# A row scale spread by two DMAs instead of transposes, plain stores in an unused path, and an earlier last block

## The chip, the cores and the metric

The kernel runs on one core of one Trainium2 chip, in float32. The metric is the device time of one execution in microseconds (us). Engines are named as in the profile: PE is TensorE, with PEld its weight loads, DVE is VectorE, ACT is ScalarE, POOL is GpSimd and SP is SyncE, which here only issues DMAs.

## The reference

Four sequences of 1024 tokens, D = 256, go through two residual blocks.

```python
x = x + _layernorm(attn_block(_layernorm(x)))
x = x + _layernorm(ffn_block(_layernorm(x)))

# attn_block
h = layer_norm(x, ln1)
q = softmax(h @ wq * scale, axis=-1)      # 4 heads of 64
k = softmax(h @ wk * scale, axis=-2)      # over the 1024 tokens
x = x + (q @ (k.T @ (h @ wv))) @ wo + bo
h = layer_norm(x, ln2)
x = x + gelu(h @ w_ff1 + b_ff1) @ w_ff2 + b_ff2
return x @ w_d + b_d

# ffn_block: nx = RMS norm of x, 8 experts, rank 16, the best 2 per token
weights = top-2 of softmax(nx @ gate.T), made to sum to 1
h1, h3 = nx @ w1.T + 2 * lora1_e(nx), nx @ w3.T + 2 * lora3_e(nx)
out = sum over experts of weight_e * ((silu(h1) * h3) @ w2.T + 2 * lora2_e(...))
```

## The kernel before

**Tiling.** The 4096 tokens are 8 blocks of 512 (BLK). A block is 4 tiles (TB) of 128 tokens, so that a tile `[128, 4, D]` holds token p, t. Two blocks make one sequence. The attention half runs per block; then tokens are scattered into DRAM rows sorted by the pair of experts that each chose, and the expert half runs over 8 groups of 512 such rows: one of kind H, six of kind F, one of kind G (n = 0 to 7). In the profiled run the attention half takes about the first 440 us, H ends near 500, the F groups near 900 and G near 972.

**Who sets the order.** The order of PE, DVE, ACT and POOL is written by the kernel itself, at build time (`manual_schedule`). The work is cut into streams, Python generators: `prelude(i)` loads a block and takes its norms, `front(i)` makes q, k and v, `middle(i)` (L846) does the residual, the second norm and the feed-forward layer, `tail(i)` (L1063 is in it) routes the tokens and scatters the rows, `prepare(n)` and `experts(n)` do an expert group. A small clock model stands beside them: `mm` and `flip` add the PE time of a matmul or transpose, `V`, `A` and `G` add a planned duration to DVE, ACT and POOL and return the planned end, and `psum` hands out the PSUM tile that is free first. A stream yields either the time at which it can go on or a condition; `side()` then picks among those that can. So a changed due time can reorder instructions far away. SP isn't part of this: its DMAs stand on one queue in an order that the framework sets, and a DMA that waits holds those behind it.

**The second norm in `middle(i)`.** After attention, `pa` is added to x1 on DVE and its mean and variance are taken; `rsqrt` (L344 on) adds eps on DVE (L348) and takes the power on POOL (L351), which gives r, one scale for each token, as a `[128, 4]` tile: tokens on partitions. The feed-forward matmuls `pf` need the norm's output with tokens along the free axis. So x1 is transposed on PE, eight flips `pt_h` (L326), which ACT copies to `x1T` in SBUF (L901). The scale of a token must then stand along the free axis on all 128 partitions: four more flips, of r broadcast along its free axis, give the PSUM tile `prb` of 128x512 (L907 to L909), and DVE multiplies (L911), twice 128x512 with one input in PSUM:

```python
prb = psum(f"prb_{i}")
for j in range(TB):
    flip(prb[:, j * P : (j + 1) * P], r[:, j : j + 1].to_broadcast([P, P]))
for c in range(DC):
    nc.vector.tensor_tensor(h2T[:, c, :], x1T[:, c, :], prb, ALU.mult)
```

A gate at L886 lets block i start its flips when block i - 2 has finished its feed-forward matmuls (`fed`), for block 7 when block 6 has, since `x1T_7` lies in the buffer "copy" of a pool with one buffer. After `pf` and gelu (L936) come the output matmuls `py`, whose result is evicted on DVE (L961).

**Other DMAs of that part.** SP loads the blocks (x at L851, z at L176), fills the DRAM rows with a default in four DMAs (`rows<-none`, L838, during block 0), and stores the routed tokens a second time into `kept` (L1127). POOL issues the indirect scatters of rows (`scatter`, L1158). In `prepare(n)` there is a pair of DMAs close to the one that the change adds: 12 rows of 128 routing values are stored to a DRAM scratch `lines` (L1206), and one of its lines is spread over 128 partitions (L1210).

**The end.** The last expert group's four output tiles go through `last` (L1448 on): for each tile j, `measured(j)` takes the norm's statistics on DVE, the power on POOL (L1463) and subtracts the mean on DVE; `stored_(j)` scales and adds the residual on DVE (L1470) and scatters the tile to the output from POOL. It is called for tiles 0 and 1 together, then for 2, then for 3 (L1652 to L1661), so that POOL's order is power 0, power 1, store 0, store 1, power 2, store 2, power 3, store 3.

**The general path.** The groups have fixed sizes. If the counts of expert pairs don't fit them, a flag is set (`have`, `both` at L978 to L980, `lack` and `short` at L1138, L1139, `flag` at L1878), and a loop under `tc.If(lacking > 0)` (L1881 on) does the expert half again on `kept`, block by block, with all experts. With these inputs it isn't taken. It is built all the same, with its own instructions for every engine, and uses `store` (L1544) and its POOL scatters.

Of the kernel before, what the change touches and what calls it, by code (L numbers as in the profile page):

```python
# [15 lines left out]
P = 128  # L16
# [10 lines left out]
TB = 4  # L27
# [39 lines left out]
def sandwich_kernel(  # L67
# [40 lines left out]
    rows = dr.tile([ROWS, RW], F32, tag="rows", name="rows")  # L108
    kept = dr.tile([NBLK * BLK, RW], F32, tag="kept", name="kept")

    lines = dr.tile([NBLK + 1, 3, BLK], F32, tag="lines", name="lines")


# [729 lines left out]

    SPARE = (2, 3, 6)
    AFTER = {4: 0, 5: 1, 6: 2, 7: 4}
    fed, turned, flipped, tails = set(), set(), set(), []  # L846

    def middle(i):
        pool, tag = (sp, "row") if i in SPARE else (xp, "x")
        xt = xts[i] = pool.tile([P, TB, RW], F32, tag=tag, name=f"x_{i}")  # L850
        nc.sync.dma_start(out=xt[:, :, 0:D], in_=tokens(x, i))  # L851
        yield now() + 2.5 if i > 1 else ARRIVE["x"]
        yield lambda: i in norms and (i - 1 in flipped if i > 1 else i == 0 or folded)
        _, r, e = rsqrt(norms[i], 1e-5, f"x{i}")
        pool, tag = (mp1, "actB") if i == 1 else (x1p, "x1")
        x1 = pool.tile([P, TB, D], F32, tag=tag, name=f"x1_{i}", bufs=1)
        yield e
        lm, e = less_mean(norms[i], r, f"x{i}")
        for j in range(TB):
            nc.scalar.activation(  # L860
                x1[:, j, :], xt[:, j, 0:D], AF.Identity, bias=lm[:, j : j + 1], scale=r[:, j : j + 1]
            )
            xe = A(0.45, e)
        nc.gpsimd.iota(xt[:, :, R_ID], pattern=[[1, TB]], base=i * BLK, channel_multiplier=TB,
                       allow_small_or_imprecise_dtypes=True)
        G(0.6)
        yield lambda: i // BPB in mixes and i in qTs
        qT, mix = qTs[i], mixes[i // BPB]
        st, mv = tiles(f"x1_{i}")
        for jj in range(0, TB, 2):  # L870
            pa = psum(f"pa_{i}_{jj}")
            for j in (jj, jj + 1):
                for c in range(DC):
                    mm(pa[:, (j - jj) * D : (j - jj + 1) * D], qT[:, c, j * P : (j + 1) * P],
                       mix[:, c, :], c == 0, c == DC - 1)
            x2 = x1[:, jj : jj + 2, :]
            nc.vector.tensor_tensor(x2, x2, pa.rearrange("p (t d) -> p t d", d=D), ALU.add)
            e = read_out(V(0.69, max(xe, now() + 0.2)))
            e = stats(x1, st, mv, (jj, jj + 1), e)
            yield 0.0  # L880
        attended.add(i)
        _, r, re = rsqrt(mv, 1e-5, f"x1_{i}", e)


        aside = {1: "u0", 3: "act", 5: "act"}.get(i)
        yield lambda: aside != "u0" or 2 in keyed and 3 in summed  # L886
        yield lambda: i < 2 or (i - 2 if i < 7 else i - 1) in fed
        yield lambda: aside != "act" or ranked.done

        if aside == "act":  # L890
            both = mp1.tile([P, 2 * DC, BLK], F32, tag="actA", name=f"x1T_{i}")
            x1T, h2T = both[:, 0:DC, :], both[:, DC : 2 * DC, :]
        else:
            (pool, tag), (pool2, tag2) = (
                ((mp2, "u0"), (mp2, "tT")) if i == 1 else ((mp1, "copy"), (bp, "h2T"))
            )
            x1T = pool.tile([P, DC, BLK], F32, tag=tag, name=f"x1T_{i}")
            h2T = pool2.tile([P, DC, BLK], F32, tag=tag2, name=f"h2T_{i}")

        def to_x1(c, pt):  # L900
            nc.scalar.copy(x1T[:, c, :], pt)  # L901

        for te in transposed(x1, f"h2_{i}", to_x1):
            yield 0.0
        flipped.add(i)
        yield re
        prb = psum(f"prb_{i}")  # L907
        for j in range(TB):
            flip(prb[:, j * P : (j + 1) * P], r[:, j : j + 1].to_broadcast([P, P]))  # L909
        for c in range(DC):  # L910
            nc.vector.tensor_tensor(h2T[:, c, :], x1T[:, c, :], prb, ALU.mult)  # L911
            e = V(0.69, max(te, now() + 0.2))
        yield read_out(e)
        yield lambda: i > 0 or once.done
        W = BLK // 2
        for hf in range(2):
            ts = slice(hf * W, (hf + 1) * W)
            gs = []
            if aside == "act":
                four = mp1.tile([P, FC // 2, BLK], F32, tag="actB", name=f"g_{i}_{hf}")  # L920
            for fp in range(FC // 2):
                pf = psum(f"pf_{i}_{hf}_{fp}")
                if aside == "act":
                    g = four[:, fp, :]
                else:
                    pool, tag = (mp2, ("yacc", "wt")[fp % 2]) if i == 1 else (gp, "g")
                    g = pool.tile([P, BLK], F32, tag=tag, name=f"g_{i}_{hf}_{fp}")
                gs.append(g)
                for k in range(2):
                    f = 2 * fp + k  # L930
                    for c in range(DC):
                        mm(pf[:, k * W : (k + 1) * W], wff1_s[:, c, f * P : (f + 1) * P],
                           h2T[:, c, ts], c == 0, c == DC - 1)
                for k in range(2):
                    f = 2 * fp + k
                    nc.scalar.activation(  # L936
                        g[:, k * W : (k + 1) * W], pf[:, k * W : (k + 1) * W], AF.Gelu_apprx_tanh,
                        bias=bff1_s[:, f : f + 1],
                    )
                    end = A(0.36, now() + 0.2, "gelu")  # L940
                read_out(end)
                if i + hf == 0:
                    prefill(fp)
                yield 0.0,

            yield end - 2.2,

            yield lambda: i == 0 or 2 * i + hf - 2 in turned
            y = x1p.tile([P, HT, DX], F32, tag="y", name=f"y_{i}_{hf}")
            sty, mvy = tiles(f"y_{i}_{hf}", HT)  # L950
            for j in range(hf * HT, (hf + 1) * HT):
                js = slice(j * P, (j + 1) * P)
                jg = slice(j % HT * P, (j % HT + 1) * P)
                py = psum(f"py_{i}_{j}")
                for c in range(DC):
                    mm(py[:, 0:DX], x1T[:, c, js], wd_s[:, c, :], c == 0, False)
                for f in range(FC):
                    o = f % 2 * W
                    mm(py[:, 0:DX], gs[f // 2][:, o + jg.start : o + jg.stop], wff2d_s[:, f, :],
                       False, f == FC - 1)  # L960
                nc.vector.tensor_tensor(y[:, j % HT, :], py[:, 0:DX], bd_s, ALU.add)  # L961
                read_out(V(0.42, now() + 0.2))
                e = stats(y, sty, mvy, (j % HT,))
                if j % HT < HT - 1:
                    yield 0.0,
            if hf == 1:
                fed.add(i)
            tails.append(Stream(always, lambda hf=hf, y=y, mvy=mvy, e=e: tail(i, hf, y, mvy, e)))
            yield 0.0

# [19 lines left out]
    def tail(i, hf, y, mv, e):  # L990
# [71 lines left out]
            return V(1.2, d, 5)  # L1062

        last = i == NBLK - 1
        yield e
        if last:
            weights()

# [240 lines left out]

    W13 = ((w1_s, b1_s), (w3_s, b3_s))  # L1310

    def experts(n, kind):
        row, to, tT, m0, m1, wt, us, ready = moe[n]
        low, high = slice(0, HALF), slice(HALF, P)
        strips = [slice(k * STRIP, (k + 1) * STRIP) for k in range(4)]
# [128 lines left out]
        def bias(j):  # L1444

            mm(share(j), ym[:, j * P : (j + 1) * P], b2_s, False, True, skip_group_check=True)

        def last(js):  # L1448

            parts = {}  # L1450

            def measured(j):

# [8 lines left out]
                e = V(0.15)  # L1462
                nc.gpsimd.tensor_tensor(r[:, 0:1], a[:, 0:1], neghalf[:, 0:1], ALU.pow)  # L1463
                G(0.6, e)
                nc.vector.tensor_scalar(o[:, j, :], share(j), mv[:, 0, 0:1], None, ALU.subtract)
                V(0.41)

            def stored_(j):

                nc.vector.scalar_tensor_tensor(  # L1470
                    o[:, j, :], o[:, j, :], parts[j][:, 0:1], row[:, j, 0:D], ALU.mult, ALU.add
                )
                e = V(0.43)
                scatter(out, to[:, j : j + 1], o[:, j, :], NBLK * BLK - 1, "out")
                G(1.1, e)

            for k, j in enumerate(js):
                measured(j)
# [22 lines left out]
        def end(jj, m):  # L1501
# [42 lines left out]
            def store(j):  # L1544
                if m == TB:
                    nc.gpsimd.tensor_tensor(o[:, j, :], o[:, j, :], row[:, j, 0:D], ALU.add)
                scatter(out, to[:, j : j + 1], o[:, j, :], NBLK * BLK - 1, "out")
                if j == TB - 1:
                    ended.add(n)

# [331 lines left out]
    with tc.If(lacking > 0):  # L1882
        with tc.For_i(0, NBLK, 1) as i:
# [2 lines left out]
            finals.clear()  # L1886
            for _ in prepare("all", "G", [(BLK, kept[bass.ds(i * BLK, BLK), :])]):
                pass
            for _ in experts("all", "G"):
                pass  # L1890
            catch_up()
            for streams in (finals, closing):
# [51 lines left out]
```

## Time and profile before

| | us |
|---|---|
| median of 3 runs | 985.9 (985.28 to 986.12) |
| the profiled execution | 985.5 |
| its span | 983.6 |
| PE busy in it | 966.5 |
| last matmul ends | 972.1 |
| last store's instruction on POOL ends | 976.0 |

The profile is of one execution. Its first part gives the busy time of each engine, the second cuts the span into 40 slices and shows each engine's busy share in tenths. Groups of instructions are named by line, engine, operation and "output<-inputs"; shapes are partitions x elements. In the timeline a line begins with its start and its busy time, and ends with the idle time of the engine ahead of it and who ended it. In the list of waits the columns are the total, the number and the longest. Matmul ends are modelled and overlap the next start, so the distance from start to start is a better price for a matmul or a flip than its busy time. PE's granted clock was 0.996 of full speed.

### The profile page before, as it was taken

To read this page: it belongs to the slowest core of one execution; us is meant where nothing else is said; L and a number is where in the kernel's file an instruction comes from. 1 tells how busy PE (TensorE), PEld (TensorE's weight loads), DVE (VectorE), ACT (ScalarE), POOL (GpSimd) and SP (SyncE) were. 2 spreads that over 40 slices of the span, in tenths; PEclk is the share of its full clock that TensorE was granted. 3 is DMA by queue.
4 is the path that set the end of the run, shared out by engine and by line. 5 is a ranking of instruction groups with operands and counts; after the bars stand their busy time and mean duration, and the time that the engine had idled before them with its cause. 6 is when DMAs were issued, how large, how long until landed. Compare 5 with 4: busy or idle time off the path is not lost. (4 is left out here: it accounts for less than half of the span.)

```text
span 983.6 us, 12174 instructions
## 1 busy us (share of the span) xinstructions
PE 966.5 (98%) x4287; PEld 651.5 (66%) x4287; DVE 457.7 (47%) x1421; ACT 337.3 (34%) x702; POOL 418.6 (43%) x468
## 2 busy tenths in 40 slices
PE   9999999999999999999999999999999999999995
PEld 7879888888888888887664463644636446374454
DVE  7677666656555455546423323333233332333133
ACT  5545544245223112311314425254252542522110
POOL 2001201201321221334745938759386593875442
PEclk9999999999999999999999999999999999999998
DMA  9514610200210110311100111102011020100000
GB/s 298 180 43 104 126 43 1 87 1 22 66 56 11 44 45 22 94 53 47 55 1 1 56 36 44 44 6 68 19 44 44 1 65 1 44 33 21 1 1 24
DMA packets 31730, 48.03 MB, mean 49 GB/s; under 512 B 4177, under 2 KB 23729, under 8 KB 31665
## 3 DMA queue, kind: packets, MB, share of 16 engines
q1 hardware_dynamic: 27072, 37.25, 13.2%
q0 software_dynamic: 3072, 8.51, 2.4%
q10 hardware_dynamic: 1520, 1.45, 0.5%
q8 instruction: 36, 0.59, 0.2%
q14 instruction: 30, 0.24, 0.1%
HBM read 26.09 MB, written 17.17 MB: 44 GB/s over the span
## 5 line engine op out<-in xcount | busy, mean ns | idle before, releaser
L313 PE MATMUL ph<-tT,w_s 128*128 128x512 f32 (+1 forms) x576 | 235.6, 554 | 1.2 <-DVE act L1348 1.0
L313 PEld LDWEIGHTS ph<-tT,w_s 128*128 128x128 f32 x576 | 105.4, 190 | 123.2 <-issue 110.8
L313 PE MATMUL py<-wff2d,g 128*128 128x264 f32 x512 | 119.2, 386 | 0.0
L313 PEld LDWEIGHTS py<-wff2d,g 128*128 128x128 f32 x512 | 97.3, 190 | 16.6
L1348 DVE TENSOR_TENSOR act<-act,ph 128x512 f32<-128x512 f32 (+1 forms) x96 | 55.7, 594 | 96.2 <-PE ph L313 52.2
L1398 POOL TENSOR_TENSOR actA<-act,act 128x512 f32<-128x512 f32 x32 | 40.7, 1272 | 128.5 <-DVE act L1348 116.0
L1699 ACT COPY py<-ph 128x512 f32<-128x512 f32 x94 | 53.2, 571 | 117.7 <-PE ph L313 116.9
L313 PE MATMUL pf<-h2T,wff_s 128*128 128x256 f32 x384 | 87.2, 380 | 0.9 <-DVE h2T L911 0.9
L1339 ACT ACTIVATE act<-ph 128x512 f32<-128x512 f32 (+1 forms) x96 | 48.4, 521 | 112.2 <-PE ph L313 91.0
L1348 DVE TENSOR_TENSOR act<-act,py 128x512 f32<-128x512 f32 x48 | 32.9, 685 | 103.6 <-ACT act L1339 103.6
L313 PEld LDWEIGHTS pf<-h2T,wff_s 128*128 128x128 f32 x384 | 71.9, 190 | 12.1 <-DVE h2T L911 1.4
L936 ACT ACTIVATE g<-pf,bff 128x256 f32<-128x256 f32 x128 | 52.0, 474 | 77.0 <-PE pf L313 62.8
L313 PE MATMUL po<-w_s,actA 128*128 128x256 f32 x256 | 60.5, 383 | 0.1
L351 POOL TENSOR_TENSOR rs_x<-rsa_x,neghalf 128x4 f32<-128x4 f32 x16 | 16.2, 1014 | 101.0 <-DVE rsa_x L348 91.3
L313 PE MATMUL po<-w_s,actB 128*128 128x256 f32 x256 | 59.2, 379 | 0.0
L1158 POOL DMA_INDIRECT rows<-x,to x32 | 32.6, 1019 | 61.0 <-DVE y L961 18.4
L313 PEld LDWEIGHTS po<-w_s,actB 128*128 128x128 f32 x256 | 48.6, 190 | 12.2 <-issue 6.2
L313 PEld LDWEIGHTS po<-w_s,actA 128*128 128x128 f32 x256 | 46.9, 190 | 12.9 <-issue 7.2
L313 PE MATMUL ph<-u,bw 32*128 32x512 f32 x192 | 54.4, 640 | 0.0
L313 PE MATMUL py<-u,bw 32*128 32x512 f32 x192 | 54.4, 640 | 0.0
L961 DVE TENSOR_TENSOR y<-py,bd_s 128x264 f32<-128x264 f32 x32 | 13.8, 431 | 80.4 <-PE py L313 80.2
L351 POOL TENSOR_TENSOR rs_y<-rsa_y,neghalf 128x2 f32<-128x2 f32 x16 | 11.3, 704 | 90.8 <-DVE rsa_y L348 81.2
(291 smaller groups left out, 1635.6 us busy)
## 6 DMA issues: line engine op xcount, KB each, us to landing
rows<-none SPq DMA_DIRECT2D x4, 1052.0 KB
kept<-x SPq DMA_DIRECT2D x8, 526.0 KB
x<-in_x_dram SPq DMA_DIRECT2D x8, 512.0 KB, 11.0
row<-rows SPq DMA_DIRECT2D x7, 526.0 KB, 4.0
z<-in_x_dram SPq DMA_DIRECT2D x6, 512.0 KB
w_s<-in_w_dram SPq DMA_DIRECT2D x3, 1024.0 KB
bw<-b_s SPq DMA_DIRECT2D x24, 128.0 KB, 4.3
wff_s<-in_wff_dram SPq DMA_DIRECT2D x2, 1024.0 KB
```

The lines of the kernel that those rows point to most:

```text
L313: nc.tensor.matmul(out_, lhsT=lhsT, rhs=rhs, start=start, stop=stop, **kw)
L351: nc.gpsimd.tensor_tensor(r, a, neghalf[:, 0:n], ALU.pow)
L936: nc.scalar.activation(g[:, k * W : (k + 1) * W], pf[:, k * W : (k + 1) * W], AF.Gelu_apprx_tanh, bias=bff1_s[:, f : f + 1],)
L961: nc.vector.tensor_tensor(y[:, j % HT, :], py[:, 0:DX], bd_s, ALU.add)
L1158: ins = nc.gpsimd.indirect_dma_start(out=dst[:, :], out_offset=bass.IndirectOffsetOnAxis(ap=at, axis=0), in_=src, in_offset=None, bounds_c ...
L1339: nc.scalar.activation(to, h, AF.Silu)
L1348: nc.vector.tensor_tensor(to, to, h3, ALU.mult)
L1398: lambda x0=x0, x1=x1, op=op: nc.gpsimd.tensor_tensor(ac, x0, x1, op))
L1699: nc.scalar.copy(py[a], ph[a])
```

## The change

It has four parts.

1. In blocks 1 to 7 the four flips of r go. r is stored by a DMA into a DRAM scratch `scales`, one 4-byte element at a time in the transposed order, and a second DMA reads the 512 values and spreads them over 128 partitions into an SBUF tile `wide`. Both are on SP. The planner counts 6.0 us for them. The product at L911 now reads SBUF for both inputs. Block 0 keeps its flips.
2. In block 7 `x1T` moves to the buffers of z, and its flips may start when all of block 6's `pf` are issued, before block 6's last `py`.
3. In `last`, the store of tile 1 is kept back until the power of tile 2 is issued; the others come where they came. The last block's rank work is planned 2.6 us later.
4. In the general path the four stores of a block are plain DMAs on SP in place of POOL's scatters.

```diff
--- before.py
+++ after.py
@@ -108,6 +108,7 @@
     rows = dr.tile([ROWS, RW], F32, tag="rows", name="rows")
     kept = dr.tile([NBLK * BLK, RW], F32, tag="kept", name="kept")
 
+    scales = dr.tile([NBLK, BLK], F32, tag="scales", name="scales")
     lines = dr.tile([NBLK + 1, 3, BLK], F32, tag="lines", name="lines")
 
 
@@ -843,6 +844,7 @@
 
     SPARE = (2, 3, 6)
     AFTER = {4: 0, 5: 1, 6: 2, 7: 4}
+    opened = set()
     fed, turned, flipped, tails = set(), set(), set(), []
 
     def middle(i):
@@ -882,9 +884,15 @@
         _, r, re = rsqrt(mv, 1e-5, f"x1_{i}", e)
 
 
+        if i:
+            wide = mp2.tile([P, BLK], F32, tag="m1", name=f"wide_{i}")
+            nc.sync.dma_start(out=scales[i].rearrange("(t p) -> p t", p=P), in_=r)
+            nc.sync.dma_start(out=wide, in_=scales[i].partition_broadcast(P))
+            re += 6.0
+
         aside = {1: "u0", 3: "act", 5: "act"}.get(i)
         yield lambda: aside != "u0" or 2 in keyed and 3 in summed
-        yield lambda: i < 2 or (i - 2 if i < 7 else i - 1) in fed
+        yield lambda: i < 2 or i - 2 in fed and (i < 7 or i - 1 in opened)
         yield lambda: aside != "act" or ranked.done
 
         if aside == "act":
@@ -892,7 +900,8 @@
             x1T, h2T = both[:, 0:DC, :], both[:, DC : 2 * DC, :]
         else:
             (pool, tag), (pool2, tag2) = (
-                ((mp2, "u0"), (mp2, "tT")) if i == 1 else ((mp1, "copy"), (bp, "h2T"))
+                ((mp2, "u0"), (mp2, "tT")) if i == 1
+                else ((zp, "z") if i == 7 else (mp1, "copy"), (bp, "h2T"))
             )
             x1T = pool.tile([P, DC, BLK], F32, tag=tag, name=f"x1T_{i}")
             h2T = pool2.tile([P, DC, BLK], F32, tag=tag2, name=f"h2T_{i}")
@@ -904,14 +913,15 @@
             yield 0.0
         flipped.add(i)
         yield re
-        prb = psum(f"prb_{i}")
-        for j in range(TB):
-            flip(prb[:, j * P : (j + 1) * P], r[:, j : j + 1].to_broadcast([P, P]))
+        if i == 0:
+            wide = psum("prb")
+            for j in range(TB):
+                flip(wide[:, j * P : (j + 1) * P], r[:, j : j + 1].to_broadcast([P, P]))
         for c in range(DC):
-            nc.vector.tensor_tensor(h2T[:, c, :], x1T[:, c, :], prb, ALU.mult)
+            nc.vector.tensor_tensor(h2T[:, c, :], x1T[:, c, :], wide, ALU.mult)
             e = V(0.69, max(te, now() + 0.2))
-        yield read_out(e)
-        yield lambda: i > 0 or once.done
+        yield read_out(e) if i == 0 else e
+        yield lambda: once.done and (i < 7 or i - 1 in fed)
         W = BLK // 2
         for hf in range(2):
             ts = slice(hf * W, (hf + 1) * W)
@@ -939,6 +949,8 @@
                     )
                     end = A(0.36, now() + 0.2, "gelu")
                 read_out(end)
+                if hf and fp == FC // 2 - 1:
+                    opened.add(i)
                 if i + hf == 0:
                     prefill(fp)
                 yield 0.0,
@@ -1062,7 +1074,7 @@
             return V(1.2, d, 5)
 
         last = i == NBLK - 1
-        yield e
+        yield e + 2.6 if last else e
         if last:
             weights()
 
@@ -1309,7 +1321,7 @@
 
     W13 = ((w1_s, b1_s), (w3_s, b3_s))
 
-    def experts(n, kind):
+    def experts(n, kind, back=None):
         row, to, tT, m0, m1, wt, us, ready = moe[n]
         low, high = slice(0, HALF), slice(HALF, P)
         strips = [slice(k * STRIP, (k + 1) * STRIP) for k in range(4)]
@@ -1445,9 +1457,16 @@
 
             mm(share(j), ym[:, j * P : (j + 1) * P], b2_s, False, True, skip_group_check=True)
 
+        parts, unsent = {}, []
+
+        def send():
+
+            while unsent:
+                j, e = unsent.pop(0)
+                scatter(out, to[:, j : j + 1], o[:, j, :], NBLK * BLK - 1, "out")
+                G(1.1, e)
+
         def last(js):
-
-            parts = {}
 
             def measured(j):
 
@@ -1462,6 +1481,7 @@
                 e = V(0.15)
                 nc.gpsimd.tensor_tensor(r[:, 0:1], a[:, 0:1], neghalf[:, 0:1], ALU.pow)
                 G(0.6, e)
+                send()
                 nc.vector.tensor_scalar(o[:, j, :], share(j), mv[:, 0, 0:1], None, ALU.subtract)
                 V(0.41)
 
@@ -1470,9 +1490,9 @@
                 nc.vector.scalar_tensor_tensor(
                     o[:, j, :], o[:, j, :], parts[j][:, 0:1], row[:, j, 0:D], ALU.mult, ALU.add
                 )
-                e = V(0.43)
-                scatter(out, to[:, j : j + 1], o[:, j, :], NBLK * BLK - 1, "out")
-                G(1.1, e)
+                unsent.append((j, V(0.43)))
+                if j != 1:
+                    send()
 
             for k, j in enumerate(js):
                 measured(j)
@@ -1544,7 +1564,10 @@
             def store(j):
                 if m == TB:
                     nc.gpsimd.tensor_tensor(o[:, j, :], o[:, j, :], row[:, j, 0:D], ALU.add)
-                scatter(out, to[:, j : j + 1], o[:, j, :], NBLK * BLK - 1, "out")
+                if n == "all":
+                    nc.sync.dma_start(out=back[j * P : (j + 1) * P, :], in_=o[:, j, :])
+                else:
+                    scatter(out, to[:, j : j + 1], o[:, j, :], NBLK * BLK - 1, "out")
                 if j == TB - 1:
                     ended.add(n)
 
@@ -1886,7 +1909,7 @@
             finals.clear()
             for _ in prepare("all", "G", [(BLK, kept[bass.ds(i * BLK, BLK), :])]):
                 pass
-            for _ in experts("all", "G"):
+            for _ in experts("all", "G", out[bass.ds(i * BLK, BLK), :]):
                 pass
             catch_up()
             for streams in (finals, closing):
```

## Prediction

> **What bounds the kernel now.** I read the page's busy shares first, then its slices, then what TensorE (PE) waited for, then the tiles the change touches, and the end of the run last.
>
> ```profile
> PE 966.5 (98%) x4287; PEld 651.5 (66%) x4287; DVE 457.7 (47%) x1421; ACT 337.3 (34%) x702; POOL 418.6 (43%) x468
> PE   9999999999999999999999999999999999999995
> ```
>
> PE is busy 98% of the span, and only the last of the 40 slices is not full: the time is the length of PE's own work, plus the few places where it waits, plus the stretch behind its last matmul. The list of PE's waits is short:
>
> ```profile
> PE pya L313 <- DVE act L1348: 1.4, 6, 0.3
> PE warm L1789 <- POOL ones L117: 1.1, 1, 1.1
> PE ph L313 <- DVE act L1348: 1.0, 1, 1.0
> PE pf L313 <- DVE h2T L911: 0.9, 1, 0.9
> ```
>
> The columns are total us, times, longest. Two single waits of about 1 us belong to the change's ground. The fourth is block 7's second norm, seen in the timeline of PE:
>
> ```profile
> 402.73 1.04 PE L326 MATMUL pt_h<-ident,x 128*128 128x128 f32 x8
> 403.61 0.60 PE L326 MATMUL prb<-ident,rs_x 128*128 128x128 f32 x4
> 405.06 1.30 PE L313 MATMUL pf<-h2T,wff_s 128*128 128x256 f32 x4 [0.85 <-DVE h2T L911]
> ```
>
> After the flips PE has nothing in its order but pf, and pf needs the product of L911. The third wait is at 478.95 in the first expert stage (H): ph waits 0.99 us for the product L1348 on VectorE (DVE), which stands behind routing work there, see (d).
>
> **The change, part by part.** Sum against the profiled run, 985.5 us (span 983.6 and 1.9 around it); it is 0.4 below the median of 985.9, so 0.4 is added at the end.
>
> (a) *28 flips go.* The row by shape:
>
> ```profile
> L326 PE MATMUL prb<-ident,rs_x 128*128 128x128 f32 x32 | 4.8, 272 | 0.0
> ```
>
> 4.8 us for 32 is 150 ns each busy; from start to start inside a group of flips I measure 109 ns in the trace. Seven blocks lose four each: 28 x 0.109 = 3.05 us, and 28 x 0.150 = 4.2 at most. They lie on PE, which has no idle time there (windows 100 to 200 and 200 to 300 are busy 100.00), so all counts. I take 3.05; no matmul is added.
>
> (b) *Two DMAs per block come, on the path from r to the product L911.* r goes to DRAM as 512 elements of 4 bytes, then a 256 KB broadcast comes back as `wide`. Before has no such pair, but the routing stage has a near one: `lines<-wt`, issue 0.31 us, next DMA that waits for its landing issued 1.3 us after it; `wt<-lines`, the same 256 KB broadcast to 128x512, issue 0.42 us and landing 3.6 us (3.5 to 3.8). Estimate from these: 0.3 + 1.3 + 0.4 + 3.6 = about 5.7 us, the planner's figure is 6.0. Upper bound: in block 1 a 1052 KB fill `rows<-none` (L838) stands on the queue between the two, and the store has 512 pieces where `lines` has 12 rows; with 5.5 us, SP's longest wait for that fill, and 2 us for slow small writes (the trace's 4-byte packets take 7 to 9 ns, so 512 on 16 engines are 0.3) it is 13 us.
> What covers it: from the last attention matmul `pa` of a block to its first `pf` the new PE order has, summed from the matmuls between, about 20 us in block 1, 25 to 50 in blocks 2 to 5, 18 in block 6 and far more in block 7. Ahead of the DMAs stand the add (0.69), the statistics (1.2), L348 (0.15) and the power on POOL (1.0): 3 us; behind them two products of 0.69. So 3 + 5.7 + 1.4 = 10.1 us against at least 18, and 17.4 at the upper bound. Cost 0 for PE. On DVE the product is queued in order and holds whatever is behind it (py's evictions, q and k of later blocks) if `wide` is late; in the new DVE order it stands 18 instructions behind L348 in block 6, 25 in block 1 and 44 to 85 in the others. Between 200 and 300 us DVE starts 236 in 100 us, one in 0.42: 7.6 us in block 6, 10.6 in block 1, 18 and more elsewhere. The power takes 1.0 of that, so the pair has 6.6 us, 9.6 and over 17. At 5.7 nothing is late; at 13 DVE stands 6.4 + 3.4 = 9.8 us in all, at worst with PE. Bounds 0 to +9.8; I take 0, as the nearest rows, `lines<-wt` and `wt<-lines` with their 5.7, have the same shape.
> SP: 14 issues at 0.3 to 0.4 us are no load on a queue whose waits run to 229 us (L1127). The two loads that could delay them, `kept` and x, wait for work that ends before r does; what stands behind a waiting pair (x and z loads) gets at most 3 us later, and the x loads already come blocks ahead.
> *A rule against this.* Trace: `both<-have,starts`, 256 numbers from SBUF twice, took 1.27 us beside a POOL product and 0.16 the other time. The Trainium skill, "SBUF — State Buffer", section "SBUF: two separate sides", says that a DVE operation with two SBUF inputs and a POOL operation reading SBUF exclude each other for their whole length; L911 read PSUM and now reads SBUF twice. If that held for every one of the 14 products, it would be up to 14 us more on DVE. Without the rule: POOL is busy 20% of 100 to 400 us, so 14 x 0.2 x half of a 1.0 us power is 1.4 us of DVE's idle time, and 0 on PE; this is what the sum has.
> *Another.* "DMA: Bandwidth & Descriptors", section "Rules for kernel authors", says that a scattered last dimension becomes one descriptor per element, and advises against it: the store of r would be 512 of them. No row of before shows such a store.
>
> (c) *Block 7's flips move up*: before block 6's last two py groups in the new order, twenty matmul calls, which are 40 records in the trace. From start to start a py record takes 222 ns (119.2 us / 512 = 233 busy), so 8.9 us of PE work lie between flips and pf. The copies and products that PE waited for now run beside it. Gain: the stall, by the timeline 403.61 + 4 x 0.109 = 404.05 to 405.06, 1.0 us (0.85 by the profile). Next late would be `wide_7`, but r of block 7 is ready long before. The DMAs that move with the freed tile (second layer's `bw` for expert stage F) are issued later yet needed only at 500 us: 0.
>
> (d) *H stage.* In the new DVE order the product that ph waited for stands ahead of routing's `both`, `have`, `lack`, `short` instead of behind. Before, these ran 475.16 to 478.57:
>
> ```profile
> 475.16 1.27 DVE L978 TENSOR_TENSOR both<-have,starts 128x2 f32<-128x2 f32 x1
> ...
> 476.54 1.24 DVE L980 TENSOR_TENSOR have<-have,both 128x2 f32<-128x2 f32 x1
> 477.81 0.17 DVE L1138 TENSOR_TENSOR lack<-have,behind 128x8 f32<-128x8 f32 x1
> ...
> 478.48 1.40 DVE L1348 TENSOR_TENSOR act<-act,ph 128x256 f32<-128x256 f32 x4
> 478.95 1.78 PE L313 MATMUL ph<-tT,w_s 128*128 128x256 f32 x7 [0.99 <-DVE act L1348]
> ```
>
> ACT had written the first part of `act` by 477.47, so DVE could start 1.0 us sooner. I take -1.0; bounds -1.0 to +1.0, as the last block's rank (held back by 2.6 in the planner) moves routing about here too.
>
> (e) *Last stores.* The timeline of POOL at the end:
>
> ```profile
> 971.09 0.59 POOL L1463 TENSOR_TENSOR rs_o<-rsa_o,neghalf 128x1 f32<-128x1 f32 x1
> 972.49 1.04 POOL L1158 DMA_INDIRECT out_dram<-tT,back  x1 [0.81 <-DVE tT L1470]
> 973.55 0.58 POOL L1463 TENSOR_TENSOR rs_o<-rsa_o,neghalf 128x1 f32<-128x1 f32 x1
> 974.94 1.04 POOL L1158 DMA_INDIRECT out_dram<-tT,back  x1 [0.81 <-DVE tT L1470]
> ```
>
> The third power's input was ready at 969.58 (L1461), but the second store held POOL to 971.07. With that store behind the power, the third store starts about 0.8 sooner, and the last power starts when its input is there (973.00 + 0.09) instead of at 973.55: -0.45 us. The last tile's matmul end (972.12) bounds it from there.
>
> (f) *General path.* It isn't run, but POOL's indirect stores in it make POOL do bookkeeping in its place. In the trace, behind the last store, POOL has a counter instruction INC_SWDGE_SEM at L1882, 976.00 to 977.45, and then DRAIN at L1940, 977.49 to 982.79; the other engines are done at 978.36 and wait for it, and 0.8 us later the run ends. With plain stores on SP the counter instruction is gone from POOL's order: -1.45 us if DRAIN only starts sooner. What DRAIN's 5.30 us are is the largest open price. The DRAIN at the program's start, before any DMA, took 0.17 us; so it has to do with POOL's DMAs. Lower end: it belongs to the counter instruction and goes too; then SP's last wait (978.36) ends the run, 4.4 us less. Upper end: it counts from the last landing (977.72), and nothing but (e) is won. I take -1.45, since the 64 indirect DMAs that POOL issues in the run itself (x32 and x32) remain for it to clear.
>
> Sum: -3.05 (a) + 0 (b) - 1.0 (c) - 1.0 (d) - 0.45 (e) - 1.45 (f) = -6.95. 985.5 - 6.95 = 978.55; with 0.4, **979.0 us**.
>
> **The rivals.**
> - *DRAIN goes with the counter.* For: it is directly behind it, and 5.3 us is out of scale with the 0.17 at the start. Against: 64 DMAs were POOL's in the run. -3.05 - 1.0 - 1.0 - 4.43 - 0.45 = -9.93: 976.0. Chance 0.24.
> - *DRAIN waits on the last store.* For: it ends 5.07 after the landing. Against: landing itself was seen by SP 5 us before. -5.5: 980.4; and if H keeps its stall, 981.4. Chance 0.17.
> - *The gain is given back* (the change doesn't do what it says): `wide` comes late and PE waits for pf or py in place of the flips. With a pair of p us the lateness is (p - 6.6) + (p - 9.6): 5 us at 10.6, 9 at 12.6, so 984 to 988. For: the chain from r grew by 5.7 us less the flips, and block 6 has 0.9 to spare. Against: PE itself has 18 us of cover, and the other five blocks are far from it. Chance 0.09.
> - *Slower*: the same queueing with a store of r drawn out to the upper bound, 13 us a pair or more. DVE holds at L911 in blocks 6 and 1 with py's and q's evictions behind it, PE's PSUM tiles fill, and all 9.8 us reach PE: 985.9 - 6.95 + 9.8 = 988.8. It decides from 12.6 us a pair. For: no 512-element store is in the trace, and block 1's pair meets a 1 MB fill. Against: `lines<-wt` lands in 1.3 us, and block 6 meets no fill. Chance 0.07.
>
> **How the numbers follow.** My forecast's own case, 978 to 980.4, has 0.43. The range 975.5 to 984.0 takes in the first two rivals and leaves out the last two. About 0.2% (2 us) is what a measurement of this kernel tells from no change: under 983.9 lie 0.43 + 0.24 + 0.17 = 0.84; within it 0.09, slower 0.07.
>
> **What would show it.** (a) x4 of prb flips instead of x32, PE busy about 963. (b) no wait of pf or py for L911 or `wide` in PE's list; landing of `wide` near 3.6 us. (c) the 0.85 gone from PE's list. (d) the wait at about 478 gone. (e) last store about 0.45 sooner behind the last matmul. (f) the stretch from the last store's end to the run's end 6.2 us instead of 7.6 (3.2 if DRAIN goes). A PE wait for L911 in several blocks would make the prediction wrong.

## The result

The changed kernel takes 990.62 us (median of 6 runs, 989.6 to 991.45), the kernel before 985.76 (6 runs): a ratio of 1.005 (95% interval 1.0039 to 1.0061). It is 4.9 us slower, where 6.95 less was forecast. The profiled execution took 990.58 us, with a span of 988.5.

The first parts of the page of after, next to those of before:

```profile
PE 966.0 (98%) x4259; PEld 649.4 (66%) x4259; DVE 459.7 (47%) x1421; ACT 340.9 (34%) x704; POOL 419.2 (42%) x468
PE   9999999999999899999999999999999999999995
```

28 matmul records are gone, as they should be, and yet the span is longer: PE waits more. One slice, the 14th, is no longer full. The list of PE's waits in after (total us, times, longest) names the places:

```profile
PE pa L314 <- DVE mix L822: 2.9, 1, 2.9
PE pf L314 <- DVE h2T L921: 1.8, 1, 1.8
PE py L314 <- ACT g L946: 1.6, 1, 1.6
...
PE pbq L314 <- DMA wq_raw<-in_wqv_dram: 1.0, 1, 1.0
PE ph L314 <- DVE act L1360: 1.0, 1, 1.0
PE ph L314 <- DVE flag_i L1903: 0.9, 1, 0.9
```

Three waits are new in the attention half (the first three), one in H (`flag_i`), the one for `act` is still there, and block 7's wait for its product is gone.

The wait for `pf` is the one that I had looked for. The timeline of after in block 1:

```profile
104.31 1.03 PE L314 MATMUL pmix<-wo_s,cbd 128*128 128x256 f32 x4
...
106.30 1.29 DVE L921 TENSOR_TENSOR h2T<-x1T,wide 128x512 f32<-128x512 f32 x2 [5.10 <-DMA wide<-scales]
...
107.13 3.23 PE L314 MATMUL pf<-h2T,wff_s 128*128 128x256 f32 x8 [1.80 <-DVE h2T L921]
```

DVE stood 5.1 us for `wide`, and PE 1.8. The eight `pf` then take 3.23 us. The windows of after show why (columns: window, its length, PE busy with matmuls, granted clock, DMA share, GB/s):

```profile
107.00:108.00 1.00, 0.87 (x3) 0.95 1.11 229
108.00:109.00 1.00, 1.00 (x4) 0.50 1.14 206
...
111.00:112.00 1.00, 1.00 (x5) 0.84 1.22 143
```

PE's clock was halved from 107.9 to 111.3 us, 3.41 us in which it does 1.7 us of work. So this one wait cost 1.8 and 1.7.

Why `wide` was late is in SP's waits, of after:

```profile
SPq L890 <- DMA scales<-rs_x: 67.9, 7, 10.6
```

The second DMA of the pair waited 67.9 us in seven blocks for the landing of the first, 9.7 each. From issue to issue that is 11.1, 10.4, 8.5, 11.0, 11.1, 8.6 and 11.0 us, where `lines<-wt` had taken 1.3. SP in block 1 of after:

```profile
88.24 0.38 SPq L889 DMA_DIRECT2D scales<-rs_x  x1
...
99.39 0.33 SPq L890 DMA_DIRECT2D wide<-scales  x1
```

And the near pair of before:

```profile
410.03 0.37 SPq L1206 DMA_DIRECT2D lines<-wt  x1
411.32 3.68 SPq L1210 DMA_DIRECT2D m<-lines  x6
```

The 4-byte packets themselves are soon under way: in block 4, 528 of them start between 227.0 and 227.5, and the second DMA is issued at 237.1. In block 1 the second DMA was late too. The product that waited for it starts 6.9 us after its issue (99.39 to 106.30), where `wt<-lines` landed in 3.6; the fills `rows<-none` are on the queue just before and behind it.

The other two waits have nothing of the scales beside them. At 164.6 us ACT is late with the gelu:

```profile
163.66 1.04 ACT L910 COPY x1T<-pt_h 128x512 f32<-128x512 f32 x2
...
164.72 1.28 ACT L946 ACT_TABLE_LOAD   x1
...
166.02 1.56 ACT L946 ACTIVATE g<-pf,bff 128x256 f32<-128x256 f32 x4
...
166.54 1.82 PE L314 MATMUL py<-wff2d,g 128*128 128x264 f32 x7 [1.60 <-ACT g L946]
```

And at 321 us `mix`, which the next attention needs, stands on DVE behind some 25 small routing instructions of another block's tail, of which two are shown:

```profile
318.56 1.11 PE L314 MATMUL pmix<-wo_s,cbd 128*128 128x256 f32 x4
...
319.43 0.73 DVE L1093 TENSOR_TENSOR count<-count,pr 128x10 f32<-128x10 f32 x4
320.07 0.19 DVE L1094 TENSOR_TENSOR rank<-pr,count 128x40 f32<-128x40 f32 x1
...
323.80 0.87 DVE L822 SCALAR_TENSOR_TENSOR mix<-pmix,ksum,bo_s 128x256 f32<-128x256 f32 x2
...
324.33 1.99 PE L314 MATMUL pa<-mix,qT 128*128 128x256 f32 x8 [2.94 <-DVE mix L822]
```

`pmix` is done at 319.7 and could be read then, but DVE gets to `mix` at 323.8.

At the end, the counter instruction of 1.45 us is gone and DRAIN takes 5.76 us in place of 5.30. From the last matmul's end to the end of the span it is 988.46 - 978.40 = 10.06 us, where before had 983.63 - 972.12 = 11.51.

### The profile page after: what moved, and what is told of

It is laid out like the page before. It is cut to its first block, busy times and chain, and to the rows that moved or that the text cites. A ratio compares the mean times of both kernels' runs of the same rounds, so it can differ in the third digit from the quotient of the medians.

```text
span 988.5 us, 12131 instructions
## 1 busy us (share of the span) xinstructions
PE 966.0 (98%) x4259; PEld 649.4 (66%) x4259; DVE 459.7 (47%) x1421; ACT 340.9 (34%) x704; POOL 419.2 (42%) x468
## 3 DMA queue, kind: packets, MB, share of 16 engines
q10 hardware_dynamic: 1520, 1.45, 0.5%
## 5 line engine op out<-in xcount | busy, mean ns | idle before, releaser
L314 PE MATMUL ph<-u,b_s 64*128 64x256 f32 (+1 forms) x192 | 46.4, 460 | 1.9 <-DVE act L1360 1.0
```

The costliest lines, as they stand in the source:

```text
L314: nc.tensor.matmul(out_, lhsT=lhsT, rhs=rhs, start=start, stop=stop, **kw)
```

## The experiments

The theory that I set out with: the loss is made of one wait for late scales, and of two waits that come from the new order alone, since the planner, told of 6.0 us and of free PE time, put the streams together anew. The rivals: all the waits come from the late scales; or parts 2 to 4 cost something too.

**No pair of DMAs, order kept (e1).**

```diff
-            nc.sync.dma_start(out=scales[i].rearrange("(t p) -> p t", p=P), in_=r)
-            nc.sync.dma_start(out=wide, in_=scales[i].partition_broadcast(P))
+            wide = wff1_s[:, 0, 0:BLK]
```

> The changed kernel without its 14 DMAs: the product L921 reads a weight tile that lies in SBUF in place of the scales, so the output is wrong in value; every engine's order stays that of the changed kernel. Theory: the profile after has three new stalls of PE, of which only the one at 105 us (1.96 us, and 1.7 us of half clock behind it) is due to the late scales; those at 164.6 (1.8) and 321 (3.1) are due to the new order on ACT and DVE. Then this kernel keeps the latter two and takes 990.6 - 3.7 = about 986.9. Rival: all three come from the late DMAs, and with them 8.5 us go: about 982. A third: none of them does, 990.6.

Measured: 988.95 us (8 runs, 986.25 to 991.68), profiled run 986.25. PE's waits in it:

```profile
PE pa L314 <- DVE mix L822: 2.9, 1, 2.9
PE py L314 <- ACT g L945: 1.6, 1, 1.6
```

The wait for the product is gone and the other two are as long as in after, without any DMA for the scales. So they belong to the order. The profiled run, in which PE's clock was not halved before the last matmul, lies 0.65 below the theory's 986.9; the median lies 2.05 above it, and only 1.7 below the changed kernel's. So the list of waits bears the theory out, and the median alone doesn't. The runs' mean granted clock goes from 0.997 at 986.25 to 0.991 at 991.68. A clock lower by 0.006 over 986 us is 5.9 us of PE work; the runs differ by 5.4. So the clock can account for the spread, though only the first of these runs was profiled.

**Contiguous store of r, order kept (e2).** The product reads the scales with a stride instead.

```diff
-            nc.sync.dma_start(out=scales[i].rearrange("(t p) -> p t", p=P), in_=r)
+            nc.sync.dma_start(out=scales[i].rearrange("(p t) -> p t", t=TB), in_=r)
...
-            nc.vector.tensor_tensor(h2T[:, c, :], x1T[:, c, :], wide, ALU.mult)
+            if i == 0:
+                nc.vector.tensor_tensor(h2T[:, c, :], x1T[:, c, :], wide, ALU.mult)
+            else:
+                by_t = lambda ap: ap.rearrange("n (t p) -> n t p", p=P)
+                nc.vector.tensor_tensor(by_t(h2T[:, c, :]), by_t(x1T[:, c, :]),
+                                        wide.rearrange("n (p t) -> n t p", t=TB), ALU.mult)
```

> The changed kernel with the store of r in the tile's own order, 128 pieces of 16 bytes in place of 512 of 4, and the product reading the scales with a stride of 16 bytes; orders unchanged. In the profile after, the spreading DMA is issued 8.5 to 11.1 us after the store, where the twelve-row store of before took 1.3. Theory: that time goes with the number of pieces, so about 3 us here, the stall at 105 goes and the time is about 987. Rival: any write of small pieces has it, so 8 to 11 us stay and the time is about 990.6.

Measured: 988.21 us (12 runs, 986.6 to 990.15), ratio to before 1.0022 (1.0013 to 1.003). From issue to issue the pair takes 1.4 to 3.1 us, and PE doesn't wait for the product. The price of the store is that of its layout, 512 pieces of 4 bytes in transposed order: 128 of 16 bytes, still small, don't have it. The number, the size and the order of the pieces changed together, so which of them it is isn't shown. The two waits of the order stay at 1.6 and 2.9, and behind the longer one the clock is halved in this profile (321.2 to 324.6), which costs 1.7 and didn't happen at this wait in after; the median is 1.2 above the theory's 987. The product takes 1.09 us in place of 0.69, which PE doesn't see.

**The pair alone (e3).** The kernel before, with part 1 of the change.

> The kernel before with the two DMAs in place of the 28 flips, and nothing else of the change. PE's order is that of the changed kernel up to block 7. Theory: the loss is all in this part: 985.8 - 3.05 for the flips + 3.7 + 1.8 + 3.1 for the three stalls + about 1 at the start or in H, so about 991 to 992.5. Rival: parts 2 to 4 cost something too, and this is 988 to 990.

Measured: 991.73 us (6 runs, 989.58 to 992.91), ratio 1.0054 (1.004 to 1.0068). Part 1 holds the whole loss. PE's list has `pa` for `mix` (2.9) and `py` for `g` (1.6) again, and `pf` for the product twice, in blocks 1 and 7. The clock is halved behind the wait for `mix` (325.2 to 328.6), not in block 1.

**Parts 2 to 4 alone (e4).** The changed kernel with the flips back in all blocks.

> The changed kernel with the flips in all blocks and no DMA for the scales: parts 2 to 4 alone. PE's order is that of the kernel before up to block 7. Theory: -1.0 for block 7's stall, -0.4 for the last stores, -1.0 for the counter instruction: about 983.3. Rival: the moved routing costs about 1 to 2 us in the first expert stage, 984.5 to 985.8.

Measured: 985.39 us (12 runs, 984.45 to 987.33), ratio 0.9998 (0.9989 to 1.0006). The rival's figure. Block 7's wait is gone, but in H PE waits 0.9 us for `flag_i`, which is new, and 1.0 for `act` as in before. The profiled run took 984.69; what puts the median 0.7 above it is not in its profile.

**Plain stores alone (e5).**

```diff
-                scatter(out, to[:, j : j + 1], o[:, j, :], NBLK * BLK - 1, "out")
+                if n == "all":
+                    nc.sync.dma_start(out=back[j * P : (j + 1) * P, :], in_=o[:, j, :])
+                else:
+                    scatter(out, to[:, j : j + 1], o[:, j, :], NBLK * BLK - 1, "out")
```

> The kernel before with plain stores in the path that isn't taken, nothing else; the orders of PE, DVE and ACT are those of before. Theory: the counter instruction of 1.45 us at the end goes and DRAIN behind it lasts about as long or 0.45 longer, as in the changed kernel: 984.2 to 984.8. Rival: what follows the last store is set by its landing, 985.7. The wait of PE for the first weight load (0.5 to 1.7 us in every kernel so far but the one before) shows here if it comes with the program's size.

Measured: 984.38 us (11 runs, 984.11 to 985.02), ratio 0.9986 (0.9977 to 0.9995): -1.4. DRAIN takes 5.76 us here too. A path that is never run cost 1.4 us.

**The planner told 14 us (e6).** `re += 6.0` becomes `re += 14.0`.

> The changed kernel with one number of the planner changed: it counts 14 us for the two DMAs in place of 6.0, near what they take (8.5 to 11.1 to the second issue, some 4 more to its landing). Theory: PE no longer waits for the scales in block 1 (-3.7), and the new order draws its own stalls; without the one at 321 it would be 983 to 986, with a like one 986 to 990. Rival: the DMAs cost what they cost wherever the product stands, 990 to 991.

Measured: 990.75 us (5 runs, 990.59 to 991.93). PE never waits for the product, nor does DVE stand for `wide`, and still the time is that of the changed kernel. The list has other waits of the order, and behind the longest the clock is halved (314.8 to 318.2), 1.7 more:

```profile
PE pa L314 <- DVE mix L822: 4.7, 2, 3.3
PE ph L314 <- DVE act L1360: 1.9, 2, 1.0
PE pr L314 <- DVE kind L1054: 1.7, 1, 1.7
```

The figure is the rival's, but not its reason: the DMAs are hidden and the order took what they had cost.

**Contiguous store, planner's number 8.0 (e7).**

> The kernel of the contiguous store with the planner's number at 8.0 in place of 6.0. In its order DVE has 6 of the routing instructions among the 25 ahead of the second sequence's last attention mix, where the changed kernel has 24 and PE waits 3.1 us. Theory: the stall at 321 comes from that place in the order alone and goes here, with the half clock behind it: about 984. Rival: that stall has to do with the scales or with the freed PE time and stays: 988.

Measured: 985.69 us (11 runs, 985.28 to 987.18), ratio 1.0 (0.9991 to 1.0009). The 2.9 us wait is gone, as is the one for `g`; two smaller waits for `mix` (2.1 in all) and two for the product (0.8) came, so that it is 2.5 below the one with 6.0 and not 4.

**The same without the delay of 2.6 us (e8).** `yield e + 2.6 if last else e` becomes `yield e`.

> As the one before, and the last block's rank isn't planned 2.6 us later. The profile after and the one of parts 2 to 4 have a new wait of 0.9 us of PE behind the flag's chain on DVE in the first expert stage, and the kernel before hasn't. Theory: the delay put it there, so 0.9 less than the run before it. Rival: it comes with plain stores or the order of the end of the attention half, no difference.

Measured: 984.95 us (11 runs, 984.52 to 985.32), 0.7 less than the run before it; the wait for `flag_i` is gone, and one of 0.7 for a routing value (`pr` for `kind`) is new. The delay had put it there.

**Parts 2 to 4 without the delay (e9).** Flips in all blocks, PE's order that of before up to block 7.

> Parts 2 to 4 without the 2.6 us delay of the last block's rank: flips in all blocks, PE's order that of before but for the end of the attention half. Theory: plain stores alone gave 984.4; block 7's earlier flips take 0.85 to 1.0 more and the store order 0.4, so about 983.2, and no wait behind the flag. Rival: H's routing waits show again elsewhere, 984 to 985.

Measured: 983.83 us (11 runs, 983.51 to 984.2), ratio 0.998 (0.9971 to 0.9989). 0.55 below plain stores alone, not 1.2: the same wait of `pr` for `kind` (0.7) is in its list. The time lies between the theory's 983.2 and the rival's 984.

**The pair in a held order, contiguous store (e10).** The planner counts the flips' PE time and PSUM tile as if they were there, and isn't told of the DMAs. Only the 28 flips leave PE's order.

```diff
+        if i:
+            wide = mp2.tile([P, BLK], F32, tag="m1", name=f"wide_{i}")
+            nc.sync.dma_start(out=scales[i].rearrange("(p t) -> p t", t=TB), in_=r)
+            nc.sync.dma_start(out=wide, in_=scales[i].partition_broadcast(P))
...
         prb = psum("prb")
-        for j in range(TB):
-            flip(prb[:, j * P : (j + 1) * P], r[:, j : j + 1].to_broadcast([P, P]))
+        if i == 0:
+            wide = prb
+            for j in range(TB):
+                flip(wide[:, j * P : (j + 1) * P], r[:, j : j + 1].to_broadcast([P, P]))
+        else:
+            pe[0] += TB * 2 * P
```

> The kernel of the run before it with the pair of DMAs in place of the flips in blocks 1 to 7, contiguous store, and the planner made to believe that the flips are still there: every engine's order stays, PE's loses the 28 flips alone. In the profile before, r is ready 9.6 us ahead of the product in block 1, 8.3 in block 4 and over 20 in the others; the pair needs 1.4 to 3.1 to the second issue and some 4 on. Theory: the loss was order and the slow store, not the idea, so the flips' 3.05 us are gained whole: 3.0 below the run before it, about 980.3. Rival: PE gains nothing as it waits for evictions and products instead (the strided product takes 1.09 in place of 0.68 us): 982 to 983.5.

Measured: 980.61 us (5 runs, 980.25 to 980.92), ratio to before 0.9945 (0.9932 to 0.9959). 3.2 us below the run before it: the flips' 3.05, whole. DVE stood 3.5 us for `wide` in block 4, where it had idled 3.4 in before, and nothing on PE waited for it. PE's waits, none of which has to do with the scales:

```profile
PE pya L314 <- DVE act L1367: 1.4, 6, 0.3
PE pbq L314 <- DMA wq_raw<-in_wqv_dram: 1.4, 1, 1.4
PE warm L1819 <- POOL ones L118: 1.1, 1, 1.1
PE ph L314 <- DVE act L1367: 1.0, 1, 1.0
PE pr L314 <- DVE kind L1061: 0.8, 1, 0.8
```

SP's wait for the store in this kernel is a seventh of that in after:

```profile
SPq L890 <- DMA scales<-rs_x: 9.3, 7, 2.8
```

This kernel beats both the one before and the changed one.

**The same held order, the change's own store (e11).**

> The same held order with the change's own store of 512 4-byte pieces. It needs 8.5 to 11.1 us to the second issue and some 4 to land, 12 to 15 in all. Theory: late by 4 to 6 us in blocks 1 and 4, where 9.6 and 8.3 are there, in time elsewhere; PE waits about that long, with 1.7 us of half clock behind such a wait at times: 7 to 13 above the contiguous one, 987 to 993. Rival: PE has other work in those blocks' order and hides it: within 2 us of the contiguous one.

Measured: 991.27 us (5 runs, 989.25 to 992.2), 10.7 above the contiguous store. The timeline of PE in it:

```profile
108.13 2.05 PE L314 MATMUL pmix<-wo_s,cbd 128*128 128x256 f32 x4 [3.11 <-DVE cbd L814]
...
271.98 3.38 PE L314 MATMUL pf<-h2T,wff_s 128*128 128x256 f32 x8 [3.33 <-DVE h2T L923]
```

Block 1 and block 4, and no other. In block 1 PE doesn't wait for the product itself, but for copies (`cbd`) that stand behind it on DVE, which stood 11.6 us for `wide`. Behind each of the two waits the clock is halved for one 3.41 us window (107.6 to 111.0 and 271.4 to 274.9): 3.1 + 3.3 + 2 x 1.7 = 9.8 of the 10.7. The two kernels differ in the store and, with it, in the product, which is the faster one here (0.69 in place of 1.09), so the 10.7 are the store's.

**The kernel before once more (e12).**

> The kernel before, unchanged, for a second profile. PE's wait for the first weight load (0.5 to 1.8 us at 6 to 8 us) is in the profile of every changed kernel and not in that of before. If it comes with the run, it can show here; if it comes with the program, it doesn't.

Measured: 985.85 us, and its list of PE's waits begins with 1.5 us for the first weight load. So that wait is of the run, not of the change, and I take it out of the comparison.

## Why the prediction was wrong

The two profiles add up. Up to the last matmul's end, after is later by 978.40 - 972.12 = 6.28 us; by the matmuls' starts, gap by gap:

| | us |
|---|---|
| (a) 28 flips | -3.05 |
| (c) block 7's wait | -1.0 |
| wait for late scales in block 1 | +1.96 |
| half clock behind it | +1.7 |
| wait for gelu at 164.6, order | +1.77 |
| wait for `mix` at 321, order | +3.1 |
| wait for `flag_i` in H | +0.9 |
| first weight load, of the run | +1.0 |
| sum | +6.4 |

The end takes back 1.45, and the span is 4.8 longer.

- **(a)** was right: 3.05 predicted, and 3.2 measured where nothing else moves (983.83 to 980.61).
- **(b) is the step that failed**, at "I take 0, as the nearest rows, `lines<-wt` and `wt<-lines` with their 5.7, have the same shape". The broadcast has; the store hasn't. `lines<-wt` writes 12 rows of 512 bytes, the new store 512 pieces of 4, and the latter takes 8.5 to 11.1 us to the next issue, not 1.3. My upper bound of 13 us for the pair had 2 us for this and 5.5 for the fill; in block 1 the pair took 18.1 from the first issue to the product. The store's time has little to do with the fill, since blocks without one have it too. But beside the fills the broadcast took 6.9 there, 3.3 above its row and more than the 1.8 that PE waited, so in block 1 both terms were at work. The 5.5 itself was misread: it is SP's wait for POOL's `none` ahead of the fill, not the fill's time. And what stood behind a waiting pair on SP was held by up to 10.6 us, not 3. The Trainium skill's rule ("DMA: Bandwidth & Descriptors", "Rules for kernel authors", one descriptor per element) stood in the prediction against the change, and I had priced it by the packets' 7 to 9 ns, and by 2 us in the upper bound. The packets were mostly as short as that, and the wait came after them.
- **(b) also lacked a term.** "Cost 0 for PE" was worked out for the wait of the product, and the new order was taken as free of stalls because the old one was. Two waits of it, 1.6 and 2.9 us, are independent of the DMAs (e1, e2), go or come with the planner's number (e6, e7), and don't exist where the order is held (e10, e11). The old order's freedom from stalls was a property of that order, not of the work. In the sum above this term is the larger one: 4.9 us for the two waits, 3.7 for the late scales. By the medians the slow store is worth 2.4 in this order (after to e2) and 10.7 in the held one.
- **(c)** was right in the profile: the wait for L911 in block 7 is gone. But in e9, which has (c) and (e), a wait of 0.7 for routing is new, and 0.55 of the expected 1.2 is left.
- **(d)** was wrong in sign. PE waits 1.0 for `act` as before, at 461 in place of 479, and 0.9 more for the flag, which the delay of 2.6 puts there (e7 to e8: -0.7).
- **(e)** was right: from the last matmul's end to the last store's start 2.82 us before, 2.40 after.
- **(f)** was right: DRAIN stays and starts sooner. It lasts 5.76 in place of 5.30, but it starts at 981.39, 0.45 before the last store's instruction ends at 981.83. From that end to DRAIN's end there are 5.31 us, where before had 6.81 with the counter instruction between: 1.5 less. Of this 0.5 is lost between DRAIN's end and the end of the span (0.84 before, 1.31 after). Plain stores alone gave 1.4 by the medians. The rival that DRAIN counts from the last landing is out: it ended 5.07 us behind that landing before, and 3.8 after.
- **The slower rival** had the mechanism of (b) and a time of 988.8, but for blocks 1 and 6. In block 6 of after DVE did stand 1.7 us for `wide`, and PE not at all; with the order held the late blocks were 1 and 4. Its chance of 0.07 was too small: the one row that spoke against it, `lines<-wt`, was the one whose shape was wrong, and the other argument, that block 6 meets no fill, had no weight, as the slow store needs no fill.
- **The first skill rule**, DVE and POOL excluding each other where both read SBUF, showed no price on DVE: the product takes 0.69 us with both inputs in SBUF, as it took 0.68 with one in PSUM (longest 0.693). But that was hardly tried, as no product of after started with more than 0.1 us of a POOL operation still to run. The other way round it shows. A power on POOL that takes 0.70 us and started 0.17 behind such a product took 1.08 in after (307.21), two in e11 1.08 each, and two in e10, beside the longer product, 1.49 and 1.50. In before, three that started beside a product with one input in PSUM took 0.70. PE waited for none of these.

What stays open: why the landing of 512 small writes comes 6.8 to 9.9 us after the last of them starts (4.2 in block 2, where their starts are spread over 6 us). The runs show that 128 pieces of 16 bytes don't have it, not at what size or number it sets in, nor whether the transposed order of the addresses has a part. And what DRAIN does in its 5.3 us was not tried.

## What to carry over

Price a DMA by a row with the same number and size of pieces, not with the same bytes: here 2 KB in 4-byte pieces took longer to land than the 256 KB broadcast with its 3.6 us. Where a planner sets the order, a change of one due time is a change of the whole order: compare with the order held before judging the idea, as the same pair of DMAs differed by 10.7 us by the layout alone (e10, e11), and the contiguous pair gave 980.6 in the held order and 988.2 in the new one, of which 0.7 is the delay. And look at what a path that isn't run leaves in the program.

## What was not expected of the hardware

**A wait of PE costs its length, or 1.7 us more.** The clock was halved for exactly 3.413 us behind some waits and not behind others of the same length. The wait for `mix` is 2.9 us in after and 2.9 in e2. In e2 it lies from 317.8 to 320.7, and the half clock starts at 321.2 and so the window before it at 317.8: all of the wait lies in one window. In after it lies from 321.4 to 324.3; by the half clock seen at 107.9, windows end every 3.413 us, one of them at 322.9: 1.5 us on one side, 1.4 on the other, and no half clock followed. In block 1 of after, 1.8 of 3.41 us idle (52%) were enough; 45% weren't. The other profiles agree but for the two ends of the run: 61% were enough in e3, 50% weren't in e6 (157.8 to 161.2), but neither were 53% at the start of e11 (5.2 to 8.6) and 56% at the end of e10 (967.4 to 970.8). So the limit lies near half a window, and isn't known closer. The Trainium skill, "TensorE: Matmul & The Clock Gate", "Part 1: The HAM clock gate (the "warmup" mystery)", has the free-running window of 3413 ns, which these runs confirm. It puts the loss of the clock after an idle window of about 3.4 us; here about half a window was enough. The runs of e1 vary with it, from 986.25 to 991.68 us; e5, e9 and e10, without a wait over 1.5 us, stay within 1 us. It isn't the whole of the spread: e4 has no long wait either and varies by 2.9.

**A store of 512 4-byte pieces** to DRAM took 8.5 to 11.1 us in after (7.9 to 12.5 in e6) from issue to the issue of what waits for it, with all its packets started in the first 1.3 to 1.8 us in six of after's seven blocks.

**A strided second input** (16 bytes from element to element) made a 128x512 product on DVE 1.09 us in place of 0.69.
